# Layer 1's dense layer by seven half-size products, and second products added in PSUM onto a copy of the first

## Chip, cores and metric

The kernel runs on one core of a Trainium2 chip. The metric is the device time of one execution in microseconds (us). A core has TensorE (PE in the profile, with its weight loads as PEld), VectorE (DVE), ScalarE (ACT), GpSimd (POOL) and SyncE (SP, which issues the DMAs here). Matmuls write PSUM, which has 8 banks; everything else on chip lies in SBUF.

## What is computed

32 independent graphs of 512 nodes with 256 features each go through four graph layers; every layer multiplies the adjacency (512 x 512) with features and passes the result through dense layers, adds the input and normalizes. Everything is fp32.

```python
# layer 0
h = (1.0 + eps) * x + einsum('bnm,bmd->bnd', adj, x)
x = layernorm(x + relu(h @ W1 + b1) @ W2 + b2)          # hidden width 512
# layer 1
h = einsum('bni,oi->bno', x, W) + b                     # 256 -> 256
h = einsum('bnm,bmo->bno', adj, h)
x = layernorm(x + where(h > 0, h, alpha * h))
# layer 2
h = layer_norm(x, gamma, beta)
conv = (adj @ h) @ W_rel + b_rel + h @ W_root
x = layernorm(x + x + relu(conv))
# layer 3
h = rmsnorm((epsilon * x + adj @ x) @ W1 + b1) * rms_w  # hidden width 1024
x = layernorm(x + silu(h) @ W2 + b2)
```

In layer 1 the kernel aggregates first: adj (x W + b) is computed as (adj x) W plus b times the row sums of adj.

## The kernel before

**Seven products.** A block product of 2 x 2 blocks is done with seven half-size products and additions instead of eight products. `aggregate` (line 973) does so for the adjacency times the features (each product two matmuls of 256 columns), `dense_feat` (1017) for the wide first dense layers of layers 0 and 3, and `dense_add` (1071) and `dense_turned` (1096) for the dense layers that end layers 0, 2 and 3. `right_sums` (886) makes four differences of the data with VectorE, `left_sums` (878) four of the other factor; for weights the latter is done once, at the start, into a constant.

All of them go through `seven(kind, ...)` (line 850), which says in what order the products are made and which PSUM bank takes each. `take` moves a bank into the result or adds it there, `put` completes a block of the result (an addition by VectorE where `more` is true, a copy otherwise):

```python
onto = kind in ONTO
y = bank(onto=onto)
product("m1", x, True)
if onto:
    copy(y, x)
else:
    take(x, 0, 0)
n = len(plan.ops)
product("m5", z, True)
if onto:
    plan.hold(n, y)
take(z, 1, 1)
product("m2", y, not onto)
put(y, 0, 0, not onto)
product("m6", x, False)
```

After that m3 goes onto z, and m7 and m4 onto x. The third argument of `product` is the start flag: without it the matmul adds to what its bank holds. `ONTO` (line 137) is empty, so m1 is taken out first and m2 goes to a bank of its own and is added to it later.

**Layer 1's dense layer.** `layer1` (1404) has two ways. With `ONE = 0` (line 135) it uses `dense_tok` (1001): for each half of the tokens a bank of two token chunks, for each chunk two matmuls of 256 columns over the two contraction chunks, 8 products a graph. VectorE then adds the bias times the row sums (`stt`, four instructions of 256 columns a graph). The way under `if ONE` (1419) writes these bias rows with ScalarE into the tile `v` and calls `dense_add` on it with kind "one".

**The order.** The program is first recorded as a list of operations with their dependencies (`Plan.add`, `Plan.do`), then `Plan.order` (483) simulates the five engines with a table of times and chooses, step by step, which operation is issued next on which engine; operations of up to five graphs (`FLIGHT`) are mixed. The result is one fixed order for each engine's queue, with semaphores between. `Pool` hands out the 8 PSUM banks and the SBUF rooms of 4 KB per partition (36, line 683); `Pool.fit` (172) admits for an added product only those banks whose columns were written as sums before. `copy` (742) may go to ScalarE or VectorE, and `YIELD` (117) is how much earlier VectorE must end for it to be chosen. `HAND` (97) is the time put down for a result to reach another engine, `GENTLE` (95) paces loads of later graphs, `AHEAD`, `RULES` and `SHIFT` (120 to 132) set how graphs follow each other. `TURN` (133) says which graphs use `dense_turned`: 3 to 28 in layer 0, none in layer 2, 1 to 28 in layer 3; the others use `dense_add`. Graph 0's first aggregation is plain (`aggregate_first`, 1363).

Of the kernel before, what the change touches and what calls it, by code (L numbers as in the profile page):

```python
# [76 lines left out]
SPARE = 1.2  # L77
# [14 lines left out]

GENTLE = 2.8

HAND = dict(tensor=0.12, vector=0.09, scalar=0.09, gpsimd=0.14, sync=0.1)
WEIGHTS, AGAIN = 0.09, 0.09


# [13 lines left out]
SOON = 0.03  # L114


YIELD = 0.9

# [2 lines left out]

RULES = [(33, 1.6, 15, 0.6)]

SHIFT = {-1: -19, 0: 12, 1: 3, 2: 5, 26: 3, 27: -1, 31: -11}  # L130
HALVES = 2
AHEAD, LAST = 93.0, 500.0
TURN = {0:(2,3),2:(99,0),3:(0,3)}
ROWS = 1
ONE = 0
PLAIN = 0
ONTO = ()
SEED = 0
BEHINDS = 1

# [144 lines left out]
class Plan:  # L285
# [191 lines left out]
    def best(self):  # L477


        rule = min(RULES, key=lambda rule: self.order(*rule)[0])  # L480
        return self.order(*rule)[1]

    def order(self, period, pace, last, near):
# [4 lines left out]
        rank = [  # L488
            (min(op.graph, final) * period + max(op.graph - final, 0) * last + SHIFT.get(op.graph, 0) + SHIFT.get(op.graph - B, 0) + n, i)
            for i, (op, n) in enumerate(zip(self.ops, need))  # L490
        ]
        tensor = sorted(r for r, op in zip(rank, self.ops) if "tensor" in op.ways)
# [9 lines left out]
        oldest, ahead, wire, lanes = 0, 0, 0.0, [0.0] * LANES  # L502
# [9 lines left out]
        while can_start:  # L512
# [52 lines left out]
            for i in can_start:  # L565
                op = self.ops[i]
# [8 lines left out]
                if op.gentle:  # L575
                    wait = max(wait, wire - GENTLE)
                at = {
                    e: max(free[e] + BEFORE * (op.crosses and not crossed), wait, ready[i][e], port[e] if op.port else 0.0) for e in op.ways
                }
                way = min(  # L580
                    at, key=lambda e: at[e] + sum(op.ways[e][0]) + YIELD * (op.yields and op.graph < B - PLAIN and e == "vector")
                )
# [6 lines left out]
            op = self.ops[i]  # L589
# [15 lines left out]
            end = t + busy + tail  # L605
# [6 lines left out]
                    port["vector"] = t + busy + PORT  # L612
            if op.wire:
                wire = max(wire, t + ADVANCE) + op.wire
                end = wire + op.late + SPARE
                if engine == "sync":
                    lanes = [*lanes[1:], end]
            for r in op.rooms:
# [9 lines left out]
            for n, result, more in op.then:  # L628
                behind[n] -= 1
                for e in ready[n]:  # L630
                    if e != engine or e != "tensor" and result:
                        ready[n][e] = max(ready[n][e], end + HAND[e] + more)
                if not behind[n]:
# [12 lines left out]
def tile_gnn_stack(ctx: ExitStack, tc: tile.TileContext, a: dict, out: bass.AP):  # L646
# [33 lines left out]
    HC = NC // 2  # L680
    TH = N // 2
    FH = FC3 // 2
    FLIGHT, ROOMS, SMALL = 5, 36, 10

    const = ctx.enter_context(tc.tile_pool(name="const", bufs=1))
    work = ctx.enter_context(tc.tile_pool(name="work", bufs=1))
# [95 lines left out]
    def bank(*shape, onto=False, sums=True):  # L782

        n = 1
        for d in shape:
            n *= d
        return Part(Room(banks, sums=n * sums, onto=n * onto)).shaped(*shape)
# [25 lines left out]
    def row(name):  # L815

        v = a[name]
        t = constant(name, [P, v.shape[0]])
        plan.move(t, v.partition_broadcast(P), v.shape[0] / 2)
        return t  # L820
# [29 lines left out]
    def seven(kind, bank, product, take, put):  # L850
# [3 lines left out]
        x, z = bank(), bank()  # L854
        onto = kind in ONTO
        y = bank(onto=onto)
# [37 lines left out]
    def weight_sums(name, a11, a12, a21, a22):  # L894

        t = constant(name, [P, 3, *a11.shape[1:]])
        left = dict(m1=a11, m2=a12, m4=a22)
        left_sums(left, a21, (a21, *(t[:, i] for i in range(3))))
        return left
# [6 lines left out]
    def blocks_of(*halves):  # L906

        return (W[:, :, i * P : (i + 1) * P] for i in range(2) for W in halves)
# [144 lines left out]
    def halves(x):  # L1053


        x = x.then(lambda v: v.rearrange("p k (h c a j) -> p h k c a j", h=2, c=HC, j=Q))
        return [x[:, h] for h in range(2)]

    def dense_sums(upper, lower):


        right = {}
        for pairs in zip(upper, lower):
            blocks = [x[h] for x in pairs for h in range(2)]
            n = blocks[0].shape[1]
            sums = right_sums(*blocks, [short(n, HC, P // Q, Q) for _ in range(3)], blocks[1])
            for m, x in sums.items():
                right.setdefault(m, []).extend(x[:, e] for e in range(n))
        return right

    def dense_add(x, right, left, done, kind="add"):


        def block(i, j):
            return x[:, j * HC : (j + 1) * HC, i * P : (i + 1) * P]

        def product(m, ps, first):
            n = len(right[m])
            for k in range(n):
                for i in range(HC):  # L1080
                    mm(
                        ps[:, i, :], right[m][k][:, i], left[m][:, k, :],
                        first and i == 0 and k == 0, k == n - 1,
                    )

        def take(ps, i, j):
            add(block(i, j), ps, block(i, j))

        def put(ps, i, j, more):
            take(ps, i, j)  # L1090
            if i == 1:
                done(j)

        seven(kind, partial(bank, HC, P), product, take, put)
# [309 lines left out]
    def layer1(x, adjacency):  # L1404
# [13 lines left out]

        if ONE:
            for c in range(NC):  # L1420
                act(v[:, c, :], b_1, AF.Copy, scale=rs[:, c : c + 1])
            dense_add(v, dense_sums(*([halves(aT[:, k : k + 1])] for k in range(DC))), A_1, done, "one")
        for h in range(0 if ONE else 2):
            if SEED:
# [119 lines left out]
    b_1 = row("L1_gnn_b")  # L1544
    if ONE:
        A_1 = weight_sums("A_1", *blocks_of(*(W_1[:, k : k + 1] for k in range(DC))))
# [71 lines left out]
```

## Time and profile before

| | us |
|---|---|
| median of 3 runs | 2281.02 (2279.61 to 2282.97) |
| the profiled execution | 2282.45 |
| its span, first to last instruction | 2280.70 |
| busy in 0 to 16 us: PE, DVE, ACT | 16.00 long: 14.81, 7.13, 3.22 |
| busy in 2265 to 2280.7 us: PE, DVE, ACT | 15.70 long: 6.74, 9.76, 12.19 |

The granted TensorE clock is 0.999 of full speed over the whole span. DMA moves 195.74 MB, 86 GB/s in the mean. In the profile almost every instruction carries line 370, the helper that issues it, so groups are told apart by engine, operation, tiles and shapes: `room` is an SBUF tile of the pool, `ps` a PSUM bank, `few` a small tile of row values, `A` the sums of weights, `L_gnn_W` and the like the weights (numbers are left out of names, so that weights of several layers share a row). For a matmul the second name after the arrow is the operand that is loaded as weights or streamed; the shape after the array size is what is streamed.

### The profile page before, as it was taken

The numbers are of one execution on the slowest core, as the hardware profiler recorded it, in microseconds if no ns is written. First come the engines' busy times: TensorE is split into PE (matmuls) and PEld (weight loads), VectorE is DVE, ScalarE is ACT, GpSimd is POOL, SyncE is SP. The second block draws the span as 40 slices with busy tenths as digits, with TensorE's granted clock in tenths as the row PEclk, the third lists the DMA queues.
The fourth block names the chain that finished last, engine by engine and source line by source line (L and its number), as shares of the span: only waits on it lengthen the run. The fifth ranks groups of instructions, "written<-read, shape, count | busy, mean of one in ns | idle before, by whom it ended". The sixth has DMA issues, their size and how long they took to land.

```text
span 2280.7 us, 37259 instructions
## 1 busy us (share of the span) xinstructions
PE 2265.3 (99%) x11694; PEld 2014.4 (88%) x11694; DVE 2120.5 (93%) x5386; ACT 1730.0 (76%) x4737; POOL 243.6 (11%) x168
## 2 busy tenths in 40 slices
PE   9999999999999999999999999999999999999998
PEld 7889888888888888888888888888888888889888
DVE  8999998999989999899999999999999999999998
ACT  4767687877887777877779777788787787678585
POOL 0101110111001010111101111101111011101011
PEclk9999999999999999999999999999999999999999
DMA  8101323233323233242332323323133323231301
GB/s 250 38 20 37 103 59 99 82 105 110 87 63 95 91 112 88 61 114 73 111 94 68 110 64 111 107 79 106 56 99 112 88 65 101 83 81 43 92 15 61
DMA packets 280503, 195.74 MB, mean 86 GB/s; under 512 B 145905, under 2 KB 225521, under 8 KB 280305
## 3 DMA queue, kind: packets, MB, share of 16 engines
q1 hardware_dynamic: 280304, 193.35, 30.1%
q8 instruction: 93, 1.52, 0.3%
q14 instruction: 106, 0.86, 0.1%
HBM read 124.27 MB, written 69.01 MB: 85 GB/s over the span
## 4 chain that ended last, share of the span: by engine, by line
PE 94%; DVE 2%; DMA 2%; ACT 1%; issue 0%; SPq 0%; POOL 0%; ACTq 0%; DVEq 0%
PE ps L370 94%; DVE room L370 2%; DMA diagonal<-room 1%; ACT room L370 1%; DMA room<-in_x_dram 0%; DMA room<-in_adj_dram 0%; DMA L_gnn_W<-in_L_gnn_W_dram 0%; SPq L417 0%; DVE few L370 0%; ACT scrap L370 0%; POOL few L370 0%; DVE few L395 0%; ACTq L1614 0%; DVE pause L1579 0%; DVEq L370 0%
## 5 line engine op out<-in xcount | busy, mean ns | idle before, releaser
L370 PE MATMUL ps<-room,room 128*128 128x256 f32 (+1 forms) x3572 | 942.2, 381 | 4.3 <-DVE room L370 3.8
L370 DVE TENSOR_TENSOR room<-room,room 128x512 f32<-128x512 f32 (+1 forms) x1486 | 859.4, 599 | 25.1 <-ACT room L370 19.3
L370 PE MATMUL ps<-room,L_gnn_W 128*128 128x256 f32 x2848 | 760.3, 379 | 0.5 <-DVE room L370 0.5
L370 PEld LDWEIGHTS ps<-room,room 128*128 128x128 f32 x3572 | 652.1, 190 | 89.6 <-DVE room L370 7.6
L370 PEld LDWEIGHTS ps<-room,L_gnn_W 128*128 128x128 f32 x2848 | 531.7, 190 | 71.5 <-DVE room L370 2.0
L370 PE MATMUL ps<-room,A 128*128 128x256 f32 x2136 | 585.2, 379 | 0.1
L370 DVE TENSOR_TENSOR room<-ps,room 128x256 f32<-128x256 f32 (+1 forms) x1125 | 517.2, 482 | 54.4 <-PE ps L370 49.4
L370 ACT ACTIVATE room<-ps,L_gnn_b_c 128x256 f32<-128x256 f32 x984 | 414.6, 470 | 111.5 <-PE ps L370 108.7
L370 POOL TENSOR_TENSOR few<-few,mhalf 128x4 f32<-128x4 f32 (+3 forms) x162 | 242.9, 1503 | 2031.5 <-DVE few L370 1356.1
L370 PEld LDWEIGHTS ps<-room,A 128*128 128x128 f32 x2136 | 399.9, 190 | 52.8 <-ACT room L370 0.4
L370 ACT ACTIVATE room<-ps 128x256 f32<-128x256 f32 x516 | 196.6, 383 | 268.6 <-PE ps L370 263.8
L370 ACT ACTIVATE room<-room,few 128x256 f32<-128x256 f32 x593 | 316.0, 595 | 28.0 <-DVE few L370 27.8
L370 DVE TENSOR_TENSOR room<-room 128x256 f32<-128x256 f32 (+1 forms) x638 | 312.0, 495 | 12.4 <-ACT room L370 8.4
L370 ACT ACTIVATE scrap<-room,few 128x256 f32<-128x256 f32 x500 | 251.4, 504 | 42.4 <-DVE few L370 36.5
L370 ACT ACTIVATE room<-room 128x1024 f32<-128x1024 f32 (+1 forms) x256 | 240.7, 951 | 29.7 <-DVE room L370 26.3
L370 ACT ACTIVATE scrap<-room 128x256 f32<-128x256 f32 x500 | 205.6, 414 | 44.9 <-DVE room L370 41.7
L370 PE MATMUL ps<-L_gnn_W,room 128*128 128x256 f32 (+1 forms) x960 | 199.5, 330 | 0.5 <-DVE room L370 0.5
L370 ACT ACTIVATE room<-room,L_gnn_rms_weight_c 128x512 f32<-128x512 f32 x256 | 174.7, 719 | 16.0 <-DVE room L370 16.0
L370 PEld LDWEIGHTS ps<-L_gnn_W,room 128*128 128x128 f32 x960 | 156.6, 191 | 15.9 <-DVE room L370 0.7
L370 PEld LDWEIGHTS ps<-A,room 128*128 128x128 f32 x1104 | 158.1, 191 | 10.9 <-DVE room L370 1.1
L370 PE MATMUL ps<-A,room 128*128 128x128 f32 x1104 | 165.0, 275 | 0.4 <-DVE room L370 0.4
L370 DVE TENSOR_TENSOR room<-room,loop 128x256 f32<-128x256 f32 (+1 forms) x256 | 105.6, 416 | 22.4 <-PE ps L370 9.9
(60 smaller groups left out, 1198.8 us busy)
## 6 DMA issues: line engine op xcount, KB each, us to landing
corner<-room SPq DMA_DIRECT2D x336, 128.0 KB, 2.5
room<-in_adj_dram SPq DMA_DIRECT2D x128, 256.0 KB, 4.5
room<-corner SPq DMA_DIRECT2D x108, 256.0 KB, 3.2
room<-in_x_dram SPq DMA_DIRECT2D x64, 256.0 KB, 5.2
out_dram<-room SPq DMA_DIRECT2D x64, 256.0 KB, 2.3
room<-corner SPq DMA_DIRECT2D x120, 128.0 KB, 3.5
room<-in_adj_dram SPq DMA_DIRECT2D x128, 64.0 KB, 2.0
diagonal<-room SPq DMA_DIRECT2D x62, 128.0 KB, 1.8
```

The costliest lines, as they stand in the source:

```text
L370: getattr(getattr(self.nc, engine), method)(to, *(put(x) for x in args), **kw)
```

## The change

`ONE` becomes 1: layer 1's dense layer goes through `dense_add` with kind "one". Its right sums are made of the aggregated features, its left sums are a new constant `A_1` of 128 x 3 x 128, made at the start from `L1_gnn_W`. `ONTO` names four kinds ("feat", the wide layers, isn't among them): in these m1 is copied from its bank into the bank of m2, and m2's matmuls add to the copy there. SBUF rooms go from 36 to 35. The constants of the planner take other values, and the planner puts down `LOADS` (2 us) more for a load of a later graph. `seven`, `dense_add`, `dense_sums` and `layer1` are unchanged; only which of their branches run.

```diff
-GENTLE = 2.8
+GENTLE = 3.2
+LOADS = 2
-HAND = dict(tensor=0.12, vector=0.09, scalar=0.09, gpsimd=0.14, sync=0.1)
+HAND = dict(tensor=0.15, vector=0.12, scalar=0.12, gpsimd=0.17, sync=0.13)
...
-YIELD = 0.9
+YIELD = 2.1
...
-RULES = [(33, 1.6, 15, 0.6)]
-SHIFT = {-1: -19, 0: 12, 1: 3, 2: 5, 26: 3, 27: -1, 31: -11}
+RULES = [(36, 1.7, 19, 0.75)]
+SHIFT = {-1: -26, 0: 12, 1: 3, 2: 2, 29: -7, 30: -11, 31: 5}
...
-AHEAD, LAST = 93.0, 500.0
+AHEAD, LAST = 88.0, 500.0
...
-ONE = 0
+ONE = 1
 PLAIN = 0
-ONTO = ()
+ONTO = ('turned','add','one','agg')
...
-                end = wire + op.late + SPARE
+                end = wire + op.late + SPARE + LOADS * op.gentle
...
-    FLIGHT, ROOMS, SMALL = 5, 36, 10
+    FLIGHT, ROOMS, SMALL = 5, 36 - ONE, 10
```

The branch of `layer1` that now runs:

```python
if ONE:
    for c in range(NC):
        act(v[:, c, :], b_1, AF.Copy, scale=rs[:, c : c + 1])
    dense_add(v, dense_sums(*([halves(aT[:, k : k + 1])] for k in range(DC))), A_1, done, "one")
```

`done` holds the activation and the normalization sums that stood behind `dense_tok` before.

## The prediction

> **What bounds the kernel now.** I read the page first: its span, the busy shares and the chain that ended last.
>
> ```profile
> span 2280.7 us, 37259 instructions
> PE 2265.3 (99%) x11694; PEld 2014.4 (88%) x11694; DVE 2120.5 (93%) x5386; ACT 1730.0 (76%) x4737; POOL 243.6 (11%) x168
> ...
> PE 94%; DVE 2%; DMA 2%; ACT 1%; issue 0%; SPq 0%; POOL 0%; ACTq 0%; DVEq 0%
> ```
>
> TensorE (PE) is busy for 2265.3 of 2280.7 us and holds 94% of the chain. Only 15.4 us are not matmul. So the time is the length of the matmul stream plus its holes, and I count matmul time first. VectorE (DVE) has 160 us in hand, ScalarE (ACT) 550.
>
> Busy time doesn't price one matmul, because records overlap. The price is the distance from start to start, and a merged row of the timeline of PE gives it: (length − duration of one) / (count − 1). Columns: start, length, engine, line, operation, shape, count.
>
> ```profile
> 1000.34 1.89 PE L370 MATMUL ps<-room,L_gnn_W 128*128 128x256 f32 x8
> ...
> 2257.69 6.19 PE L370 MATMUL ps<-L_gnn_W,room 128*128 128x128 f32 x54
> ...
> 2264.61 5.08 PE L370 MATMUL ps<-A,room 128*128 128x128 f32 x44
> ```
>
> With 0.379 us for one 256-column record: (1.89 − 0.379)/7 = 0.2159 us. With 0.275 for one of 128 columns: (6.19 − 0.275)/53 = 0.1116, and (5.08 − 0.275)/43 = 0.1117. Half the columns cost 0.517 of the time, weights loaded anew each time.
>
> Third, the groups by shape (busy and mean ns of one, then idle time before):
>
> ```profile
> L370 PE MATMUL ps<-L_gnn_W,room 128*128 128x256 f32 x512 | 136.9, 379 | 0.0
> ...
> L370 DVE TENSOR_TENSOR room<-ps,room 128x256 f32<-128x256 f32 x837 | 330.0, 413 | 26.1 <-PE ps L370 22.7 <-ACT room L370 0.4 <-ACT scrap L370 0.2
> ...
> L370 DVE TENSOR_TENSOR room<-room,room 128x256 f32<-128x256 f32 x446 | 182.9, 412 | 1.6 <-ACT room L370 0.6 <-DMA room<-in_x_dram 0.3
> ...
> L370 DVE SCALAR_TENSOR_TENSOR room<-L_gnn_b,few,ps 128x256 f32<-128x256 f32 x128 | 56.2, 473 | 1.2 <-PE ps L370 0.8
> ...
> L370 ACT ACTIVATE room<-ps 128x256 f32<-128x256 f32 x512 | 194.2, 382 | 268.5 <-PE ps L370 263.8 <-DVE room L370 3.1
> ...
> L370 ACT ACTIVATE room<-shift_rel,few 128x256 f32<-128x256 f32 x128 | 55.8, 506 | 5.5 <-DVE few L395 5.5
> ```
>
> The first row is layer 1's dense product: 512 instructions = 32 graphs x 8 products x 2, so each fp32 product is two instructions. The copies out of PSUM are all on ACT, which spent 263.8 us waiting for PE ahead of them: it is early there, not late.
>
> Fourth, the waits of PE and of its weight loads, and two stretches (from:to and length, then busy of PE, PEld, DVE, ACT, POOL, clock, DMA share, GB/s):
>
> ```profile
> PE ps L370 <- DVE room L370: 5.2, 8, 1.6
> PE ps L370 <- ACT room L370: 0.5, 1, 0.5
> ...
> PEld ps L370 <- DVE room L370: 12.9, 30, 2.0
> PEld ps L370 <- ACT room L370: 3.4, 9, 0.9
> ...
> 50.00:100.00 50.00, 48.84 (x272) 43.10 (x271) 49.04 (x144) 37.09 (x112) 4.31 (x3) 1.00 0.12 38
> ...
> 200.00:400.00 200.00, 198.43 (x1013) 175.98 (x1013) 185.41 (x473) 147.46 (x399) 20.64 (x13) 1.00 0.28 76
> ...
> 1000.00:1200.00 200.00, 200.00 (x1009) 178.09 (x1008) 187.57 (x475) 153.92 (x426) 21.94 (x14) 1.00 0.33 93
> ```
>
> In the middle there are no holes; from 200 to 400 us, the worst full stretch, 1.57 us. Of the 15.4 us, 1.2 precede the first matmul and 8.45 follow the last (it ends at 2272.25), so 5.8 us of holes lie between.
>
> **The change, part by part.**
>
> *Matmuls of layer 1.* Removed per graph: 8 products of 256 columns, 16 instructions x 0.2159 = 3.454 us. Added: seven half products, each of 2 token chunks and 2 contraction chunks folded into one sum, so 14 products of 128 columns, 28 x 0.1116 = 3.125 us. Saved 0.329 us a graph, x 32 = **−10.5 us**. Bounds: the 128-column rows agree within 0.0001 us, and mixed with longer ones a pair also takes 0.22; so −10 to −11.
>
> A rule speaks against this. The Trainium skill, "TensorE: Matmul & The Clock Gate", Back-to-back issue gap, says that in streams of weight load and matmul the load counts, and gives 81 ns at 128 columns and 131 at 512. An estimate from that page: a quarter of the columns costs 0.62, half of them no less, so 28 x 0.62 x 0.2159 = 3.75 us a graph, 0.29 more than before, and the kernel would be 9 us slower instead of 10.5 faster. The two 128-column rows above, streams with a load per matmul, show 0.517 and decide.
>
> *Adding onto a copy.* In every aggregation but graph 0's first (127), 54 "turned" dense layers (26 of layer 0, 28 of layer 3) and 42 "add" ones (6, 32 and 4 in layers 0, 2, 3), one DVE add of 256 from PSUM goes: 223. Its place takes an ACT copy PSUM to PSUM; with layer 1's own 32 there are 255 copies. No matmul is added.
>
> *DVE.* Gone: 128 scalar_tensor_tensor (56.2 us) and 223 adds. New in layer 1: 4 subtractions and 6 adds per graph, 128 and 192. Adds from PSUM: 837 − 223 + 192 = 806. By busy time over count (0.394 for adds, 0.410 for subtractions): −56.2 − 31 x 0.394 + 128 x 0.410 = −16 us; DVE stays near 92%. The larger YIELD can move 47 more small jobs to ACT, which only eases DVE.
>
> *ACT.* +128 scaled bias rows, by the shift_rel row 0.506 each = 65; +255 copies. No row writes PSUM from ACT; nearest are ACT out of PSUM, 382 ns, and with a bias 470. I take 382: 97 us; by 470, 120. ACT rises from 1730 to about 1892 us (83%), 1915 at the most. Hidden under PE, as its 263.8 us of waiting for PE shows; without that cover all 162 would come on top.
>
> *The new wait.* m2 can't start before the copy of m1 is done, with m5 between (0.86 us in an aggregation, 0.45 in layer 1). On PE's queue everything planned after m2 stands behind it, whatever graph it is of; ACT and DVE wait for those. Before, 319 groups of seven (127 + 54 + 42 + 96 of the wide layers) had 4 bank reuses each, 1276 waits of one kind, and left 5.8 us of holes: 4.5 ns each. New are 255 + 32 x 4 = 383: x 4.5 = **+1.7 us**. From above, all PE and weight-load waits shown (22.0 us, 17 ns each): +6.6. Nothing excludes 0. I take 1.7, since holes, not loads' waits, lengthen the stream.
>
> *Waits that go.* DVE caused 18.1 of the 22.0, so about 4.8 of the holes; 223 of its 1125 adds from PSUM (20%) go: **−1.0** (0 to −4.8).
>
> *Start.* A_1 takes 4 DVE operations of 128 columns, about 0.29 each, 1.2 us, in a stretch where DVE is busy 49.04 of 50 and PE idles 1.16: **+0.3** (0 to 1.2).
>
> *Settings and rooms.* GENTLE, LOADS, HAND, RULES, SHIFT, AHEAD and one room less issue nothing, yet the whole order is made anew. DMAs are the same in number. Worst: every 200 us like 200 to 400, 11.4 x 1.57 = 17.9, +12.1. Best: all holes gone, −5.8. DMA is about a third busy, and PE has no wait for a load after the start; I take **0**, both signs being open.
>
> **Sum:** −10.5 + 1.7 − 1.0 + 0.3 = −9.5 us. The profiled execution took 2282.45 us (1.75 beyond its span), so 2272.9; the median of the runs shown is 1.43 lower, so **2271.5 us** there. Its own range is 2267 to 2276.
>
> **Rivals** (a difference under 0.2%, 4.6 us, can't be told from none here).
>
> *Better order:* the new settings close the holes as well. For: they are local, 1000 to 1200 us has none. Against: 9.6 us at start and end don't move. 2281.0 − 10.5 − 4.5 = 2266. Chance 0.14.
>
> *Gain eaten:* one room less, three more half rooms in layer 1 and a third bank held through m5 leave fewer choices, and half of the bound on the order (+6) comes true: 2278. Chance 0.10.
>
> *The copy becomes the bound (slower):* m2 stands at PE's head until ACT has read and written; ACT's 1024-wide jobs take 1.06 us and run in order. PE's 8 shown waits for DVE were 0.65 us each. 16 such waits, one in 16 copies, take the 10.5 us; 24, one in 11, make it slower than the bound; one in 7 gives 36 x 0.65 = 23 us, 2294. Against: ACT is early at PSUM, and other graphs fill the gap between m5 and m2. Chance 0.08.
>
> *No gain from halves:* the saving isn't there because weight loads (190 ns each, 111 ns apart) limit the stream once strided chunks are the weights: +0 and the waits, 2282 or, by 0.12 a matmul instead of 0.1116, 28 x 0.12 = 3.36 and 2279. The A rows, which have such chunks, speak against. Chance 0.03.
>
> **How the numbers follow.** The forecast has 0.65. Faster by over 0.2% means below 2276.5: forecast 0.64, better order 0.14, a little of the eaten gain: 0.80. Within: 0.10. Slower: 0.10 (copy 0.08, the rest of order). The range goes from all holes closed, 2264.5, to 2280, past the eaten gain; beyond lies about 0.15.
>
> **What would show it.** Layer 1's row of 512 256-column matmuls gone and 896 of 128 columns at 0.112 apart; PE busy about 2254.8; adds of 256 from PSUM 806; 255 ACT copies from PSUM to PSUM under 0.47 us; PE's waits for ACT below 5 us. Wrong if 200 us stretches in the middle show PE below 199, or PE's waits for ACT exceed 10 us.

## The result: slower by 0.4%, and the profile after

The changed kernel takes 2291.16 us (median of 5 runs, 2289.71 to 2292.51) against 2281.19 us for the kernel before (5 runs): a ratio of 1.004, 95% interval 1.0027 to 1.0052. Forecast was a gain of 9.5 us; it lost 10.

The page of the changed kernel, its span, busy times and the chain that ended last:

```profile
span 2289.1 us, 38367 instructions
PE 2262.9 (99%) x12078; PEld 2017.4 (88%) x12078; DVE 2103.9 (92%) x5313; ACT 1859.0 (81%) x5143; POOL 240.6 (11%) x168
...
PE 84%; DMA 5%; DVE 5%; ACT 4%; SPq 2%; issue 1%; POOLq 0%; POOL 0%; ACTq 0%; DVEq 0%
```

TensorE is still busy for 99% of the span, but it holds 84% of the chain, not 94%, and DMA and SP's queue, which had 2% together, have 7%. The groups by shape hold the parts of the change:

```profile
L371 PE MATMUL ps<-A,room 128*128 128x128 f32 x1488 | 216.8, 275 | 1.1 <-DVE pause L1580 1.0
L371 PE MATMUL ps<-L_gnn_W,room 128*128 128x128 f32 x960 | 143.1, 275 | 0.7 <-DVE room L371 0.5 <-ACT room L371 0.2
...
L371 DVE TENSOR_TENSOR room<-ps,room 128x256 f32<-128x256 f32 x806 | 324.5, 413 | 27.4 <-PE ps L371 24.2 <-ACT room L371 1.0
...
L371 ACT ACTIVATE ps<-ps 128x256 f32<-128x256 f32 x255 | 94.3, 371 | 96.5 <-PE ps L371 95.9 <-DVE room L371 0.3
...
L371 ACT ACTIVATE room<-L_gnn_b,few 128x256 f32<-128x256 f32 x128 | 55.1, 500 | 3.8 <-DVE few L396 3.5 <-PE ps L371 0.2
```

The two matmul rows of the same names and shape in the kernel before:

```profile
L370 PE MATMUL ps<-A,room 128*128 128x128 f32 x1104 | 165.0, 275 | 0.4 <-DVE room L370 0.4
...
L370 PE MATMUL ps<-L_gnn_W,room 128*128 128x128 f32 x448 | 63.6, 275 | 0.5 <-DVE room L370 0.5
```

The 512 matmuls of 256 columns are gone; 384 (1488 − 1104) and 512 (960 − 448), that is 896, of 128 columns have come. The work is what the diff says.

So the loss is in holes of the matmul stream. I measure a hole as the distance from one matmul's start to the next beyond 0.2159 us (256 columns) or 0.1116 (128), and add up those over 0.05 us, by stage of the run (us, one profiled execution each):

| kernel | 0–100 | 100–200 | 200–600 | 600–1800 | 1800–2100 | later | all |
|---|---|---|---|---|---|---|---|
| before | 5.1 | 0.4 | 3.1 | 1.2 | 2.4 | 1.5 | 13.6 |
| changed | 3.9 | 5.7 | 9.0 | 10.0 | 3.7 | 1.2 | 33.6 |

Matmul work −10.5, holes +20, and the stretch after the last matmul 1.5 us shorter (8.45 to 6.95): +8, and the span grew by 8.4. The new holes come mainly at two places: one at 151 us, and many small ones from 200 to 1800 us.

Matched with the planner's list, the holes of the middle stand ahead of two products of layer 2: m4 of its aggregation (25 holes, 10.8 us over the run) and m1 of its dense layer (14 holes, 5.7 us, of which the largest, 2.7 us at 338 us, is PE's own wait for a transfer). The kernel before has no hole over 0.05 us ahead of either. One of the holes ahead of m4, in the timelines of the changed kernel (start, length, engine, line, operation, and in brackets the idle time before it and what ended it), first SP's queue, then VectorE, then PE:

```profile
1523.18 2.74 SPq L418 DMA_DIRECT2D corner<-room  x4
1526.40 0.83 SPq L418 DMA_DIRECT2D room<-corner  x2
1527.29 1.15 SPq L418 DMA_DIRECT2D out_dram<-room  x2
1528.49 1.64 SPq L418 DMA_DIRECT2D room<-in_adj_dram  x3
1530.17 1.87 SPq L418 DMA_DIRECT2D room<-corner  x4
```

```profile
1539.01 0.69 DVE L371 TENSOR_TENSOR room<-room 128x512 f32<-128x512 f32 x1 [1.11 <-DMA room<-corner]
```

```profile
1541.70 1.56 PE L371 MATMUL ps<-room,room 128*128 128x256 f32 x6 [0.64 <-DVE room L371]
```

The first row writes the pieces of layer 2's transposed h to memory, the last row of SP reads them back in four quarters (`gather_squares`). Between them SP issues two writes of results and three loads of a later graph's adjacency, 256 KB each. The fourth quarter, issued at 1531.61, lands 7.28 us later (a piece of the chain); VectorE's next instruction needs it, and everything queued behind that one waits with it, also the additions out of PSUM that PE's next products wait for. The same place in SP's queue in the kernel before:

```profile
1017.25 2.74 SPq L417 DMA_DIRECT2D corner<-room  x4
1020.10 4.42 SPq L417 DMA_DIRECT2D room<-corner  x6
1025.00 3.30 SPq L417 DMA_DIRECT2D out_dram<-room  x2
1028.36 1.87 SPq L417 DMA_DIRECT2D room<-in_adj_dram  x4
```

Results and loads follow the quarters here. By the planner's lists, over the whole program no load and no result of the kernel before stands between pieces and quarters of any graph; in the changed kernel 75 loads and 49 writes of results do. The transfers of 600 to 1800 us, with the median time to landing, first before, then changed:

```profile
room<-corner SPq DMA_DIRECT2D x72, 128.0 KB, 3.5
```

```profile
room<-corner SPq DMA_DIRECT2D x68, 128.0 KB, 6.5
```

and VectorE's waits for them in that stretch (total, times, longest), again before, then changed:

```profile
DVE room L370 <- DMA room<-corner: 1.8, 3, 0.9
```

```profile
DVE room L371 <- DMA room<-corner: 12.4, 18, 1.9
...
PEld ps L371 <- DVE room L371: 10.6, 12, 1.5
PE ps L371 <- DVE room L371: 6.1, 9, 1.1
```

The Trainium skill, "DMA: Bandwidth & Descriptors", Queues, rings and completion order, says that each DMA engine takes the descriptors of one issuing queue in ring order. This trace agrees: of the transfers shown, the three loads landed at 1535.0, 1536.1 and 1537.4 us, the four quarters after them, from 1537.9 to 1538.9.

### The profile page after: what moved, and what is told of

Its sections match the earlier page's. It is cut to its first block, busy times and chain, and to the rows that moved or that the text cites. A ratio compares the mean times of both kernels' runs of the same rounds, so it can differ in the third digit from the quotient of the medians.

```text
span 2289.1 us, 38367 instructions
## 1 busy us (share of the span) xinstructions
PE 2262.9 (99%) x12078; PEld 2017.4 (88%) x12078; DVE 2103.9 (92%) x5313; ACT 1859.0 (81%) x5143; POOL 240.6 (11%) x168
## 4 chain that ended last, share of the span: by engine, by line
PE 84%; DMA 5%; DVE 5%; ACT 4%; SPq 2%; issue 1%; POOLq 0%; POOL 0%; ACTq 0%; DVEq 0%
PE ps L371 84%; DVE room L371 4%; DMA room<-corner 4%; ACT room L371 3%; SPq L418 2%; ACT scrap L371 1%; DMA room<-in_x_dram 1%; DMA out_dram<-room 0%; DVE few L371 0%; DMA corner<-room 0%; DVE few L396 0%; DVE pause L1580 0%; DVE A L371 0%; DVE L_gnn_W_root L371 0%; POOLq L1615 0%
## 5 line engine op out<-in xcount | busy, mean ns | idle before, releaser
L371 PE MATMUL ps<-room,room 128*128 128x256 f32 (+1 forms) x3572 | 925.8, 381 | 7.9 <-DVE room L371 7.6
L371 DVE TENSOR_TENSOR room<-room,room 128x512 f32<-128x512 f32 (+1 forms) x1550 | 878.9, 592 | 7.8 <-DMA room<-corner 3.3
L371 PE MATMUL ps<-room,L_gnn_W 128*128 128x256 f32 x2848 | 772.5, 380 | 0.7 <-DVE room L371 0.5
L371 PE MATMUL ps<-room,A 128*128 128x256 f32 x2136 | 570.7, 379 | 3.7 <-ACT room L371 3.7
L371 DVE TENSOR_TENSOR room<-room 128x256 f32<-128x256 f32 (+1 forms) x702 | 338.8, 486 | 32.8 <-DMA room<-corner 16.2
L371 ACT ACTIVATE room<-room 128x1024 f32<-128x1024 f32 (+1 forms) x256 | 241.3, 946 | 18.4 <-DVE room L371 13.1
L371 PEld LDWEIGHTS ps<-A,room 128*128 128x128 f32 x1488 | 209.7, 192 | 16.6 <-DVE room L371 1.2
L371 PE MATMUL ps<-A,room 128*128 128x128 f32 x1488 | 216.8, 275 | 1.1 <-DVE pause L1580 1.0
L371 ACT ACTIVATE ps<-ps 128x256 f32<-128x256 f32 x255 | 94.3, 371 | 96.5 <-PE ps L371 95.9
L371 PEld LDWEIGHTS ps<-L_gnn_W,room 128*128 128x128 f32 x960 | 138.6, 191 | 10.8 <-DVE room L371 0.7
L371 PE MATMUL ps<-L_gnn_W,room 128*128 128x128 f32 x960 | 143.1, 275 | 0.7 <-DVE room L371 0.5
```

What stands on the lines that cost most here:

```text
L371: getattr(getattr(self.nc, engine), method)(to, *(put(x) for x in args), **kw)
```

## The experiments

Theory: the new order of SP's queue makes layer 2's quarters late, and VectorE passes this on to PE. Rivals: the new waits of m2 and the longer hold on PSUM; the start; the added work itself. The edits below keep the order that the planner wrote for the changed kernel, apart from what they move (but for the two that say otherwise). Each was run beside the kernel before on the same chip.

**Loads behind the quarters.**

```diff
-        return self.order(*rule)[1]
+        return loads_behind(self.order(*rule)[1])
```

`loads_behind` goes through the list and holds every adjacency load that comes between a graph's pieces and its quarters back until after the last quarter.

> The changed kernel (2291.2 us), every engine's order kept, but adjacency loads of later graphs that SP issues between the two halves of layer 2's transposition through memory (pieces written, quarters read back) are put behind the quarters. Theory late quarters: three or four 256 KB loads ahead of them make the quarters land 7 us after their issue instead of 2.3, VectorE stands at the first instruction that needs them, and PE waits behind it before layer 2's products, 10.9 us before m4 of its aggregation and 5.6 before m1 of its dense layer. Then the quarters land within 4 us, these holes shrink by 8 to 13 us, and the kernel takes 2278 to 2283 us. Rival new waits (m2 after the copy, banks held longer): nothing moves, 2289 to 2292 us. Rival loads needed so early: the loads are late now, 2292 us or more.

2283.90 us against 2279.62: ratio 1.002 (1.0011 to 1.0029), half of the loss. The holes of 600 to 1800 us went from 10.0 to 1.4 us, and the median quarter lands after 4.2 us, not 6.5. (The 2.3 us of the expectation isn't what the kernel before shows: its median is 3.5.) But 10.7 us now lie in 1800 to 2100 us, the largest (3.7 us) where VectorE waits for an adjacency load: among the last graphs the loads have no time to spare. The theory holds for the middle; its size was spoilt at the end.

**Small loads.**

```diff
+                n = 64 if b > 7 else N
-                plan.move(self.chunk(m), a["adj"][b][:, m, :], LOAD, gentle=b > 0)
+                plan.move(self.chunk(m)[:, 0:n], a["adj"][b][:, m, 0:n], LOAD, into=self.chunk(m), gentle=b > 0)
```

> The changed kernel, order kept, but from graph 8 on each adjacency load brings 64 of 512 columns only (an eighth of the bytes, the rest of the tile keeps what an earlier graph left). If the bytes of the loads hold the quarters up: quarters land within 3.5 us, holes in layer 2 go, 2278 to 2283 us, like with the loads behind. If it is the place in SP's queue and its issue time alone (0.5 us a load): no more than 2 us gained, 2289 us. Rival new waits: 2289 to 2292 us.

2276.64 us against 2279.62, ratio 0.9985 (0.9977 to 0.9994). The loads still stand ahead in the queue, each with its issue; the quarters of 600 to 1800 us land 3.2 us after theirs:

```profile
room<-corner SPq DMA_DIRECT2D x72, 128.0 KB, 3.2
```

Only 0.6 us of hole is left in that stretch. So it is the bytes of the loads ahead that delay, not their place and issue time alone.

**Loads behind, up to graph 26.**

```diff
-        if waiting and op.gentle and (op.wire, op.late) == LOAD:
+        if waiting and max(waiting) < 27 and op.gentle and (op.wire, op.late) == LOAD:
```

> As with all loads behind the quarters, but the last graphs keep the old order: only where the quarters are those of graphs up to 26. With all of them moved, the holes of 600 to 1800 us fell from some 12 to 1.4 us, and new ones of 3.7 and 1.3 us came after 1900 us, where VectorE waited 5.9 us for loads of the adjacency. Theory late quarters: the gain stays and these go, 5 to 7 us less than with all moved: 2276 to 2279 us, level with the kernel before or up to 3 us below it. Rival loads needed early: moved loads cost in the middle too, 2282 us or more.

2278.36 us against 2280.78, ratio 0.9988 (0.9979 to 0.9997): all of the loss is gone, with every instruction of the change in place, the longer hold on PSUM included. The waits of 600 to 1800 us:

```profile
DVE room L399 <- DMA room<-in_adj_dram: 2.1, 3, 0.8
DVE room L399 <- DMA room<-corner: 1.0, 2, 0.6
PE ps L399 <- DVE room L399: 0.9, 3, 0.4
```

VectorE's 12.4 us of waiting for quarters are down to 1.0, and PE's 6.1 for VectorE to 0.9. The holes of the whole run fall from 33.6 to 19.5 us; 5.7 us of them still lie at 100 to 200 us, where the kernel before has 0.4. The forecast gain isn't reached: by medians the kernel is 2.4 us below the one before. (Its trace is of the fastest of 11 executions, 2276.71 us, so its holes may be a little on the low side.)

**No wait for the copy.**

```diff
-            copy(y, x)
+            aside(y, x)
...
-        product("m2", y, not onto)
+        product("m2", y, True)
```

`aside` makes the same ScalarE copy, in the same place of the queue, into a spare SBUF tile.

> The changed kernel, order kept, but the copy of m1 goes to a spare SBUF tile and m2 starts its bank afresh, so that m2 no longer waits for the copy (what m1 gives to that block is left out). The prediction put this new wait at 1.7 us (0 to 6.6). Theory late quarters: the wait costs PE next to nothing, 0 to 2 us less than the changed kernel's 2291. Rival new waits, the cause of the loss: 8 us or more less, 2283 us or below.

2288.72 us against 2280.78, ratio 1.003 (1.002 to 1.004), where the changed kernel has 1.004 and, run again, 1.0034 (1.0021 to 1.0046). The holes are 32.7 us, not 33.6, and VectorE waits 13.1 us for quarters. The rival falls as the cause of the loss: the new wait costs 0.5 to 2 us, hardly beyond what the runs can tell.

**Old settings.** The kernel before with `ONE = 1`, the four kinds in `ONTO` and 35 rooms, and nothing else.

> Both parts of the change with the planner's old settings. Theory the order sets the time: the old settings fit the old list of operations only; the planner itself counts an end at 2469 us for it, so 2460 to 2490 us, with PE holes of over 150 us that start at once in the plan. Rival the new settings lose what the parts gain: about 2270 us, as the matmuls alone say.

2475.06 us against 2280.78 (2 runs), ratio 1.085. The planner's count was right to 0.3%. The settings aren't a part of the change that could be left out; they are the search for an order, and each fits one list of operations. For the same reason neither part was run alone: with the new settings the planner itself counts 2364 us without `ONTO` and 2312 without `ONE`, and such a run would have measured an order. What one part alone gives with an order of its own stays open.

**Traffic in the kernel before.**

```diff
+            if (op.wire, op.late) == QUARTER and op.graph not in met:
+                met.add(op.graph)
+                if 5 < op.graph < 27:
+                    for m in range(3):
+                        nc.sync.dma_start(extra[m], a["adj"][op.graph][:, m, :])
```

> The kernel before, whose quarters have no load ahead of them, with three transfers of 256 KB (adjacency to a spare place in HBM) issued ahead of the quarters of graphs 6 to 26; nothing waits for them. Theory late quarters: transfers ahead are enough to make the kernel before slow too; quarters land 6 to 8 us after issue, and as its order doesn't allow for them, 3 to 5 us of hole in each of 21 graphs: 2340 to 2385 us, with the holes before layer 2's products. Rival, the loss belongs to the added copies and the seven products: 2281 to 2286 us.

2290.59 us (2 runs) against 2280.07, ratio 1.0046 (1.0028 to 1.0065). The direction is as expected, the size far smaller: 10 us, as much as the change itself lost. VectorE waits for the quarters in 600 to 1800 us:

```profile
DVE room L370 <- DMA room<-corner: 23.6, 14, 3.5
```

but the stretch has only 9.4 us of holes, where the kernel before has 1.2. I had counted the delay in full for each of 21 graphs; 14 waits were seen in this stretch (18 in the whole run), and PE went on during more than half of their time. The median quarter lands after 5.3 us here, not 3.5. Three transfers ahead of the quarters are enough to make the kernel before as slow as the changed one, with none of its new work. They are additional traffic, though (63 transfers of 256 KB), and not all of the new holes stand before layer 2: ahead of m4 of its aggregation there are 6.7 us over the run, but ahead of the first product of layer 0's aggregation 3.8 us, against 0.9 before.

**Results behind, too.** With both moves (below) and

```diff
-        if waiting and max(waiting) < 27 and op.gentle and (op.wire, op.late) == LOAD:
+        if waiting and max(waiting) < 27 and op.gentle and (op.wire, op.late) in (LOAD, RESULT):
```

> As the run with both moves, and the two 256 KB writes of results that still stood ahead of the quarters are put behind them as well. Theory late quarters: the remaining 3.5 us before m4 of layer 2's aggregation go, quarters land within 3 us: 2 to 3 us less than with both moves. Rival: two writes ahead stay within the slack that the order leaves, no difference beyond 1 us.

2287.16 us against 2280.07, ratio 1.0031 (1.002 to 1.0043): worse by 8 us, which neither side had foreseen. The waits of 600 to 1800 us say why:

```profile
DVE room L417 <- DMA room<-in_adj_dram: 9.2, 16, 2.0
...
DVE room L417 <- DMA room<-corner: 0.2, 1, 0.2
```

The quarters are in time (median landing 3.2 us), and now the loads, which stand behind the results, are late. The queue has due times on both sides.

**The start.** Three runs went after the hole at 151 us. It is in the planner's own list: 4.2 us at 152.7 us, ahead of the same product (m3 of the wide layer of layer 0 of graph 3), where the list of the kernel before has no hole between 100 and 200 us. Here PE's timeline in the changed kernel, and the busy times of 100 to 200 us with the clock:

```profile
146.17 1.03 PE L371 MATMUL ps<-room,L_gnn_W 128*128 128x256 f32 x4
150.88 1.51 PE L371 MATMUL ps<-room,A 128*128 128x256 f32 x4 [3.69 <-ACT room L371]
152.19 1.91 PE L371 MATMUL ps<-room,L_gnn_W 128*128 128x256 f32 x4
...
100.00:200.00 100.00, 96.31 (x529) 86.49 (x529) 90.65 (x235) 77.94 (x209) 6.67 (x6) 0.98 0.15 36
```

After 3.69 us of standing still, four matmuls take 1.91 us instead of 4 x 0.216 plus the last one's 0.16: the granted clock is 0.98 over 100 to 200 us, where it was 1.00 before, so the hole costs about 2 us more than its own length (5.7 us in the table's column of 100 to 200 us).

First the two ScalarE copies that it waits for, moved ahead (`earlier` puts an operation of the list right behind the last one that it depends on or that uses the same room):

```diff
-        return self.order(*rule)[1]
+        return earlier(self.order(*rule)[1], (1674, 1675))
```

> The changed kernel, order kept, but the two ScalarE copies of graph 3 for which PE stands 3.85 us at 150.9 us (m3 of the wide layer of layer 0) are issued right after the last use of the SBUF room that they write, ahead of four other ScalarE instructions. Theory ScalarE's order at the start: the hole shrinks by 2 to 3 us, and the slow clock after it (1.9 us) may go: 2286 to 2289 us. Rival room: the copies had to wait for a room, and PE can't go on much earlier: less than 1 us, 2290 to 2292 us.

2287.97 us against 2279.62, ratio 1.0036: no gain that can be told. The hole, 3.7 us long, stood one product later, ahead of m4 of the same layer, and waited for VectorE's addition.

Then with that addition, and the loads behind up to graph 26, `loads_behind(earlier(self.order(*rule)[1], (1674, 1675, 1689)))`:

> Loads behind the quarters up to graph 26, and at the start the two ScalarE copies of graph 3's m5 moved ahead as before, now with the VectorE addition that stands behind them (the run with the copies alone had its 3.7 us hole one product later, waiting for that addition). Theory: hole at 150 us falls from 3.9 to under 2 us and the slow clock after it goes, 2 to 4 us less than with the loads alone (2278.4): 2274 to 2277 us. Rival: graph 0's chain in layer 3 is then what PE waits for, 2277 to 2279 us.

2279.28 us against 2280.07, ratio 0.9998 (0.9989 to 1.0007). The hole is 3.87 us and stands before layer 1's m3:

```profile
152.87 1.51 PE L414 MATMUL ps<-A,room 128*128 128x128 f32 x3 [3.87 <-DVE room L414]
```

Last with layer 1's bias rows and the additions onto them, too:

```diff
-        return loads_behind(earlier(self.order(*rule)[1], (1674, 1675, 1689)))
+        return loads_behind(earlier(self.order(*rule)[1], (1674, 1675, 1689, 1273, 1274, 1271, 1272, 1284, 1290)))
```

> Loads behind the quarters up to graph 26, and at the start all that PE was seen to wait for in turn is moved as early as the SBUF rooms allow, ahead of graph 0's last squares: the copies and the addition of graph 3, the four new bias rows of layer 1 in graph 2 (kind one) and the two additions onto them. With the first three alone the hole was 4.0 us and stood before layer 1's m3. Theory order of the queues at the start: the hole falls below 2 us and the slow clock after it goes, 3 to 5 us less than with the loads alone (2278.4): 2273 to 2276 us. Rival rooms: these instructions start when graph 0 gives its rooms back, at 148 to 149 us, and something else stops PE: 2277 to 2280 us.

2282.64 us against 2279.97, ratio 1.0011 (1.0001 to 1.002), worse than with the loads alone:

```profile
151.24 1.04 PE L414 MATMUL ps<-A,room 128*128 128x128 f32 x6 [1.47 <-DVE room L414]
157.20 1.22 PE L414 MATMUL ps<-room,L_gnn_W 128*128 128x256 f32 x2 [4.91 <-ACT room L414]
```

It was 3.7 us long before one product, 3.9 before another, now 1.5 and 4.9 before two. So it isn't one badly placed instruction that PE waits for: each time the wait was found again at the next product. The first instructions of each moved group write rooms that graph 0 gives back between 148 and 149 us by the plan's count, and the others follow on them; whether the rooms or the backlog of ScalarE and VectorE is the limit wasn't told apart and stays open.

**Up to graph 24, beside the changed kernel.**

> Loads behind the quarters only up to graph 24 (to 26 it left 1.0 us of hole at 1809 us, where VectorE waited 1.3 us for a moved load of graph 27). Theory late quarters, with loads that have a due time too: 0 to 1.5 us less than the 2278.4 of the run up to 26, and 1 to 4 us below the kernel before. Rival: the gain on the kernel before does not come again, 2280 us or more.

> The changed kernel unchanged, on the same chip as the run with loads behind up to 24, so that the two stand side by side: 9 to 11 us above the kernel before, 11 to 14 us above the other run.

2279.26 us and 2289.05 us against 2280.54: ratios 0.9997 (0.9988 to 1.0006) and 1.0034 (1.0021 to 1.0046). On one chip the moved loads are worth 9.8 us. The limit at 24 is no better than at 26; level with the kernel before is what is certain, and the run up to 26, 0.1% below it, is the fastest that does the whole work.

## Why the prediction was wrong, point by point

**Matmuls of layer 1: right.** 896 for 512, and the distances hold: a stretch of four such matmuls at 141.82 us lasts 0.61 us, (0.61 − 0.275)/3 = 0.112 apart, and over all 896 the median distance is 0.111. With this price the account of matmuls, holes and tail closes to 0.4 us of the span's growth, so the gain of 10.5 us is there and the holes eat it. The rule weighed against it, that weight loads would set the pace at 128 columns, doesn't bind here.

**Copies, VectorE, ScalarE: right in kind, ScalarE too high.** 255 copies at 371 ns (382 taken), 806 additions, VectorE −16.6 us (−16 forecast); ScalarE 1859 us where 1892 was forecast (+129 for +162; the bias rows took 55.1 us, not 65, as their records overlap). The Trainium skill, "ScalarE: Activation LUTs", Step-by-step, has ScalarE faster to PSUM than to SBUF: 371 against 377 ns for the copies of the same shape into SBUF in this profile, a difference that decides nothing.

**The new wait: right in size.** 1.7 us forecast; holes 0.9 us less without it, and 0.5 to 2 us of time, hardly beyond the runs' spread. Its base was low, though: by distances of starts the kernel before has 13.6 us of holes, not the 5.8 that busy times leave. The slower rival, the copy as the bound, named the wrong mechanism for the right sign.

**Waits that go: not seen in the changed kernel.** Instead of 1.0 us less of holes, PE's and its weight loads' waits for VectorE rose from 18.1 us to 26.9. With the adjacency loads behind the quarters up to graph 26 they are 12.2, so in the changed kernel VectorE's own waiting may hide what the term forecast.

**Start, +0.3: not seen.** 0 to 100 us has 3.9 us of holes, 5.1 before.

**Settings and rooms, taken as 0: the step that failed.** It read "DMA is about a third busy, and PE has no wait for a load after the start". Both are true of the kernel before, and neither answers the question. A late transfer reaches PE mostly through VectorE, which stands in order at the first instruction that needs it: in the whole changed run VectorE waits 19.6 us for the quarters, PE itself 4.0 us in three waits. The view to open was the waits of VectorE for DMAs, and next to it the order of SP's queue around the quarters: 1.8 us of waiting in 1200 us, with results and loads just behind, suggests that the old order hits its due times closely and that a new one may miss them. The measured price: the holes grew by 20.0 us, of which the moved loads take 14.1 back and 5.3 lie at 100 to 200 us (5.7 against 0.4); in time, the moved loads are worth 9.8 us on one chip, and the start stays unmended. Which of the settings put the loads there, or whether any order of the new list must, stays open. The rival "gain eaten" had a worse order for its cause, but 6 us of it, a third of what came; the stated range, up to 2280, ends 11 us below the measured time. The prediction's own sign of being wrong came: of the 200 us stretches in the middle, 1000 to 1200 us shows PE at 198.2.

**The planner's own count** would have been a second warning: the last operation of its list starts at 2273.0 us before and at 2273.1 after the change. So the order for 10.5 us less work came with 11 us more holes in the plan itself (19.3 against 8.0, most of the difference in the first 200 us, the hole at 151 us among them). The other 9 us, in layer 2, the plan didn't have: it counts no hole there between 600 and 1800 us.

## What to carry to other kernels

When a change lets a planner make a whole order anew, the sum of the added and removed work says little: ask what in the old order was only just in time, and price its loss. Look for late transfers at the engine that consumes them, however idle the DMA engines are in the mean: a short read that another step waits for must not stand behind long loads that nobody waits for yet, and a load moved behind it has a due time of its own. Where a hole moves to the next product each time the instruction that it waited for is put earlier, as here three times, moving single instructions doesn't mend it.

## What the runs showed that I had not expected

The size of what a few 256 KB transfers do to four reads of 128 KB behind them, though DMA is a third busy in that stretch. The median landing of the quarters: 3.5 us in the kernel before, 3.2 in the changed one with neither loads nor results ahead, 4.1 with results alone, 6.5 with both, and 3.2 with both where the loads have an eighth of their bytes. And how much of a late transfer PE can hide: with 23.6 us of VectorE's waiting for quarters in 600 to 1800 us the kernel before, with the transfers added, had 9.4 us of holes; with 12.4 us the changed one had 10.0. Why it hides less wasn't tested.
